# Head sums of layer 1 in three batches: by ScalarE's relu and an adding DMA in place of VectorE

## The chip, the core and the metric

The kernel runs on one core of a Trainium2 chip. Its engines are TensorE (PE in the profile, its weight loads PEld), VectorE (DVE), ScalarE (ACT), GpSimd (POOL) and SyncE (SP, which only issues transfers). Each works through its own instructions in order and waits on semaphores for the others. The metric is the device time of the whole kernel in microseconds, lower is better.

## The reference

Sixteen graphs (batches) of 1024 nodes with 128 features pass through two layers of graph attention. The change is in layer 1, whose computation is this:

```python
# x: [16, 1024, 128], adj: [16, 1024, 1024], H = 4 heads
h = jnp.einsum('bnf,hfd->hbnd', X, conv_w) + conv_b[:, None, None, :]
scores = jnp.einsum('hbni,hij,hbmj->hbnm', h, attn_w, h)
Ah = jnp.tanh(A[None] * scores)
hh = jax.nn.relu(jnp.einsum('hbnm,hbmd->hbnd', Ah, h))
Xm = jax.nn.relu(jnp.mean(hh, axis=0))
return jax.nn.relu(Xm + X)
# and around it: x = _layernorm(x + layer1(x, adj))
```

The mean over the four heads of the relu of each head's output is what this case is about. Layer 0 (masked softmax attention with three gates, then a layer norm) runs ahead of layer 1 for the next batch.

## The kernel before

Everything is 32-bit float. Layer 1 of one batch is 32 steps: 4 heads (hd) times 8 blocks of 128 nodes (m). A step s is 8*hd + m. `layer1_step` does the following in step s.

- TensorE multiplies a block of x1T with uT into two PSUM tiles `sc` of 128x512 (L704). The tag `sc` has four PSUM slots, which small tiles of layer 0 use as well.
- VectorE multiplies each with the adjacency into the SBUF tile `s`, 128x1024, of tag `s1` with four slots (L705).
- ScalarE takes the tanh of `s` in place (L706).
- TensorE accumulates the `s` of two steps earlier, with h1 as weights, into the PSUM tile `acc1`, 128x1024 (L710). The function `back` that does so waits in a list, `pending`, of length DELAY = 2. Tag `acc1` has one slot: the next head's accumulation starts after the last reader of this head's.
- After the last block of a head, which is two steps into the next head (or batch), `back` calls `add_head` for each half of 512 columns. For head 0 it writes relu(acc) into the SBUF tile `sum` (L726), for the others it adds relu(acc) to it (L728). Head 0 thus ends at step 9, head 1 at step 17, head 2 at step 25, and head 3 at step 1 of the next batch.

At step 2 of the next batch `layer1_end` transposes `sum` on VectorE (L281), writes it to DRAM and reads it back in another order through SP's queue (L263, L268), then adds x1 (L774, L775), normalises and stores the rows. `sum` has one buffer.

The order of everything is written out by hand: tables named BETWEEN and AHEAD tell after which step which piece of layer 0 of the next batches is emitted. What matters here: step 14 to 20 hold the score blocks S of layer 0 two batches ahead (L354 on TensorE, L360 on ScalarE) with their transpositions T (L378), and the gates of the next batch (sum L549 on VectorE, product L543 on GpSimd); step 25 transposes the next batch's x1 (L281) and starts the adjacency loads L0 to L7, one per step, on GpSimd's queue (L302); then come edges E (L401 on GpSimd), masks A (L418 and L426 on VectorE, the exponential L430 on ScalarE) and weightings B (L444, L451 on VectorE, L448 on ScalarE, L462 on TensorE). GpSimd issues the adjacency loads and the output stores; SP issues the rest. A slot of a tag is handed to a new tile when all reads of the old one are behind it in the program, and the first instruction that touches the new tile waits for them to be done.

Of the kernel before, what the change touches and what calls it, by code (L numbers as in the profile page):

```python
# [11 lines left out]
F32 = mybir.dt.float32  # L12
BF16 = mybir.dt.bfloat16
U8 = mybir.dt.uint8
AF = mybir.ActivationFunctionType
ALU = mybir.AluOpType
# [3 lines left out]
P = 128  # L20
# [4 lines left out]
def two_layer_adjacency_kernel(  # L25
# [19 lines left out]
    nc = tc.nc  # L45
# [9 lines left out]
    sb = ctx.enter_context(tc.tile_pool(name="sb", bufs=2))  # L55
# [631 lines left out]
    def layer1_step(b, hd, m):  # L687
# [20 lines left out]
        def back(halves=range(NH)):  # L708
            for q in halves:
                nc.tensor.matmul(  # L710
                    acc[:, ts(q, 512)], h1[:, ts(hd, D)], s[:, ts(q, 512)],
                    start=(m == 0), stop=(m == NB - 1),
                )
            if m == NB - 1:
                if hd == 0:
                    sum_t[b] = sb.tile([P, N], F32, tag="sum", name=f"sum_{b}", bufs=1)
                for q in halves:
                    add_head(b, hd, acc[:, ts(q, 512)], q * 512)
# [3 lines left out]
    def add_head(b, hd, a, at):  # L722

        o = sum_t[b][:, at : at + a.shape[1]]
        if hd == 0:
            nc.vector.tensor_scalar_max(o, a, 0.0)  # L726
        else:
            nc.vector.scalar_tensor_tensor(o, a, 0.0, o, op0=ALU.max, op1=ALU.add)  # L728
# [142 lines left out]
    for b in range(B):  # L871
        plan = BETWEEN if b else {**BETWEEN, **FIRST}
        after = layer0(b + 2) if b + 2 < B else {}
        for step in range(H * NB):
            hd, m = divmod(step, NB)
# [81 lines left out]
```

## Time and profile before

| what | value |
|---|---|
| runs | 2409.5, 2409.74, 2414.6 us; median 2409.74 |
| profiled execution | span from first to last instruction 2407.4 us; its own device time is not listed apart, the median run lies 2.3 us above the span |
| busy | PE 2398.8 us, DVE 1551.3, ACT 1063.5, POOL 608.9 |
| one batch in the steady part | 148.77 us |
| L728, add of a head's half on VectorE | 95 times, 686 ns each |
| L726, head 0's half | 32 times, 686 ns each |
| GpSimd's issue of a load of 512 KB | 590 ns; 4.1 us from issue to landing |
| granted TensorE clock | 0.999 of full speed |

How to read it: busy times are sums over the span, per engine, and say which engine has room. A line of the groups names the source line, engine, operation, what it writes and reads, how often, its busy time and mean, and then the idle time of its engine just before it with what ended that idle time. A timeline line gives the start and length in us, the engine, the line and the operation, and in brackets the idle time before it. Windows give the busy time of each engine in a stretch, then the clock, the share of time in which the 16 DMA engines were busy, and GB/s.

### The profile page before, as it was taken

To read this page: it belongs to the slowest core of one execution; us is meant where nothing else is said; L and a number is where in the kernel's file an instruction comes from. 1 tells how busy PE (TensorE), PEld (TensorE's weight loads), DVE (VectorE), ACT (ScalarE), POOL (GpSimd) and SP (SyncE) were. 2 spreads that over 40 slices of the span, in tenths; PEclk is the share of its full clock that TensorE was granted. 3 is DMA by queue.
4 is the path that set the end of the run, shared out by engine and by line. 5 is a ranking of instruction groups with operands and counts; after the bars stand their busy time and mean duration, and the time that the engine had idled before them with its cause. 6 is when DMAs were issued, how large, how long until landed. Compare 5 with 4: busy or idle time off the path is not lost.

```text
span 2407.4 us, 20166 instructions
## 1 busy us (share of the span) xinstructions
PE 2398.8 (100%) x5983; PEld 1095.6 (46%) x5983; DVE 1551.3 (64%) x3262; ACT 1063.5 (44%) x1503; POOL 608.9 (25%) x389
## 2 busy tenths in 40 slices
PE   9999999999999999999999999999999999999999
PEld 5444444444444444444444444444444444444444
DVE  7666666766667656666666666667666576666555
ACT  6545344453444534445444454444444344443333
POOL 2214131241312313133131231313214132141000
PEclk9999999999999999999999999999999999999999
DMA  5334151442414324243242422425234252341010
GB/s 192 72 78 123 46 130 42 97 106 50 126 47 104 94 60 115 53 111 82 63 113 62 115 69 70 110 56 123 62 78 108 51 131 53 80 115 34 18 27 10
DMA packets 474194, 196.98 MB, mean 82 GB/s; under 512 B 414948, under 2 KB 440291, under 8 KB 474084
## 3 DMA queue, kind: packets, MB, share of 16 engines
q1 hardware_dynamic: 455501, 129.03, 23.0%
q0 software_dynamic: 18288, 66.59, 9.3%
q8 instruction: 48, 0.79, 0.1%
q14 instruction: 63, 0.51, 0.1%
q10 hardware_dynamic: 294, 0.07, 0.0%
HBM read 136.12 MB, written 59.51 MB: 81 GB/s over the span
## 4 chain that ended last, share of the span: by engine, by line
PE 99%; DVE 1%; ACT 0%; issue 0%; POOLq 0%; DVEq 0%
PE sc L704 36%; PE acc L710 36%; PE acc L462 9%; PE sc L354 5%; PE pR L675 5%; PE pT_u L238 5%; PE pR_h L335 1%; PE pT_q L238 1%; PE acc_other L462 0%; PE idle L136 0%; DVE R L418 0%; DVE s L705 0%; PE pt L496 0%; DVE st L214 0%; PE turn L371 0%
## 5 line engine op out<-in xcount | busy, mean ns | idle before, releaser
L705 DVE TENSOR_TENSOR s<-sc,adj 128x512 f32<-128x512 f32 x1008 | 685.1, 688 | 713.9 <-PE sc L704 692.7
L706 ACT ACTIVATE s<-s 128x1024 f32<-128x1024 f32 x504 | 533.1, 1058 | 1056.9 <-DVE s L705 897.7
L704 PE MATMUL sc<-uT,x1T 128*128 128x512 f32 x2048 | 962.8, 592 | 0.2
L710 PE MATMUL acc<-s,h 128*128 128x512 f32 x2016 | 947.3, 592 | 0.0
L710 PEld LDWEIGHTS acc<-s,h 128*128 128x128 f32 x2016 | 380.5, 190 | 484.7 <-issue 476.7
L704 PEld LDWEIGHTS sc<-uT,x1T 128*128 128x128 f32 x2048 | 386.7, 190 | 470.2 <-issue 403.5
L401 POOL TENSOR_SCALAR edge<-adj 128x1024 uint8<-128x1024 f32 x120 | 332.8, 2773 | 315.3 <-DVE top_None L418 312.9
L218 POOL TENSOR_TENSOR rs<-rs,mhalf 128x8 f32<-128x8 f32 (+3 forms) x35 | 54.2, 1549 | 881.0 <-DVE rs L217 880.9
L462 PE MATMUL acc<-R,hz 128*128 128x512 f32 x492 | 231.6, 592 | 0.2 <-ACT hz L448 0.2
L430 ACT ACTIVATE R<-R,nmax 128x1024 f32<-128x1024 f32 x126 | 144.6, 1147 | 81.0 <-DVE nmax L426 73.3
L418 DVE CUSTOM_DVE_ANT_0 R<-R,edge 128x1024 f32<-128x1024 f32 x126 | 152.8, 1213 | 0.5 <-ACT hz L448 0.5
L451 DVE TENSOR_TENSOR R<-R,adj 128x1024 f32<-128x1024 f32 (+1 forms) x127 | 152.0, 1197 | 0.0
L462 PEld LDWEIGHTS acc<-R,hz 128*128 128x128 f32 x492 | 93.1, 190 | 115.7 <-issue 111.4
L354 PE MATMUL sc<-xT,qT 128*128 128x512 f32 (+3 forms) x384 | 144.9, 486 | 0.0
L360 ACT ACTIVATE R<-sc,h 128x512 f32<-128x512 f32 (+1 forms) x192 | 111.1, 580 | 52.3 <-PE sc L354 46.8
L543 POOL TENSOR_TENSOR x1T<-hp,wu_b 128x1024 f32<-128x1024 f32 x45 | 106.4, 2363 | 103.8 <-DVE hws L549 63.6
L238 PE MATMUL pT_u<-x1T,ms 128*128 128x512 f32 x256 | 120.6, 593 | 0.0
L675 PE MATMUL pR<-cw,x1T 128*128 128x512 f32 x256 | 117.6, 598 | 0.0
L354 PEld LDWEIGHTS sc<-xT,qT 128*128 128x128 f32 x384 | 69.9, 190 | 70.0 <-issue 60.6
L302 POOL DMA_DIRECT2D adj<-in_adjT_dram x112 | 66.1, 590 | 91.8 <-DVE s L705 91.8
L728 DVE SCALAR_TENSOR_TENSOR sum<-acc,sum 128x512 f32<-128x512 f32 x95 | 61.2, 686 | 41.7 <-PE acc L710 41.7
L678 ACT COPY h<-pR 128x512 f32<-128x512 f32 x128 | 72.4, 593 | 28.2 <-PE pR L675 26.4
(163 smaller groups left out, 1151.5 us busy)
## 6 DMA issues: line engine op xcount, KB each, us to landing
adj<-in_adjT_dram POOLq DMA_DIRECT2D x112, 512.0 KB, 4.1
xT<-in_xT_dram SPq DMA_DIRECT2D x16, 512.0 KB, 4.7
adj<-in_adjT_dram SPq DMA_DIRECT2D x16, 512.0 KB, 8.8
x<-in_x_dram SPq DMA_DIRECT2D x16, 512.0 KB, 5.5
dram_hp<-turn_hp SPq DMA_DIRECT2D x15, 512.0 KB, 2.6
hp<-dram_hp SPq DMA_DIRECT2D x60, 128.0 KB, 3.1
dram_x<-turn_x SPq DMA_DIRECT2D x15, 512.0 KB, 2.9
x1T<-dram_x SPq DMA_DIRECT2D x60, 128.0 KB, 5.5
```

Source lines behind the costliest of these rows:

```text
L238: nc.tensor.matmul(ps, w, src[:, ts(q, 512)], start=True, stop=True)
L354: nc.tensor.matmul(ps[:, : at - lo], t["qT"][:, ts(j, P)], t["xT"][:, lo:at], start=True, stop=True)
L401: engine.tensor_scalar(m, adj_t[b, j], 0.0, None, ALU.is_gt)
L418: nc.vector.tensor_tensor_reduce(to[:, ks], s[:, ks], t["edge", j][:, ks], 1.0, nmax, ALU.mult, ALU.max, top)
L430: nc.scalar.activation(row(j), row(j), AF.Exp, bias=t["nmax", j], accum_out=t["z", j])
L451: nc.vector.tensor_mul(s[:, ks], s[:, ks], adj[:, ks])
L462: nc.tensor.matmul(t["acc"][q], t["hz", j], row(j)[:, ts(q, BH), :], start=(j == 0), stop=(j == NB - 1),)
L675: nc.tensor.matmul(ps, x1T_t[b][:, ts(k, P)], cw.rearrange("p h d -> p (h d)"), start=True, stop=True)
L704: nc.tensor.matmul(ps, x1T[:, ts(m, P)], uT[:, ts(q, 512)], start=True, stop=True)
L705: nc.vector.tensor_mul(s[:, ts(q, 512)], ps, adj[:, ts(q, 512)])
L706: nc.scalar.activation(s, s, AF.Tanh)
L710: nc.tensor.matmul(acc[:, ts(q, 512)], h1[:, ts(hd, D)], s[:, ts(q, 512)], start=(m == 0), stop=(m == NB - 1),)
```

## The change

In batches 9, 10 and 11, for heads 1, 2 and 3, `add_head` no longer lets VectorE add. ScalarE writes relu(acc), 128x512, from PSUM into a new SBUF tile `r`, and GpSimd issues a DMA that adds `r` to the half of `sum`. `r` takes a slot of tag `s1`, the four slots that `s` uses; `r` fills half of one. Head 0 and all other batches are as before.

```diff
--- before.py
+++ after.py
@@ -722,6 +722,11 @@
     def add_head(b, hd, a, at):
 
         o = sum_t[b][:, at : at + a.shape[1]]
+        if hd and b in (9, 10, 11):
+            r = sb.tile([P, 512], F32, tag="s1", name=f"r_{b}_{hd}_{at}", bufs=4)
+            nc.scalar.activation(r, a, AF.Relu)
+            nc.gpsimd.dma_start(o, r, accum_op=ALU.add)
+            return
         if hd == 0:
             nc.vector.tensor_scalar_max(o, a, 0.0)
         else:
```

## The prediction

> **What bounds the kernel now.** I read the page's busy shares first, then its chain of waits, then the costliest groups.
>
> ```profile
> PE 2398.8 (100%) x5983; PEld 1095.6 (46%) x5983; DVE 1551.3 (64%) x3262; ACT 1063.5 (44%) x1503; POOL 608.9 (25%) x389
> PE 99%; DVE 1%; ACT 0%; issue 0%; POOLq 0%; DVEq 0%
> L728 DVE SCALAR_TENSOR_TENSOR sum<-acc,sum 128x512 f32<-128x512 f32 x95 | 61.2, 686 | 41.7 <-PE acc L710 41.7
> ```
>
> TensorE is busy throughout and the chain is 99% PE. The list of waits between 1334 and 1930 us shows no wait of PE's matmuls at all, and head 1 of batches 9, 10 and 11 reaches L728 at 1486.32, 1635.09 and 1783.85: 148.77 us apart each time, so one batch stands for all three. The times below are batch 9's. Freeing VectorE (64%) buys nothing by itself. The question is whether the change delays anything that PE needs.
>
> [...]
>
> **What goes and comes.** In batches 9 to 11, heads 1 to 3, two halves: 18 instructions of L728 leave DVE (18 x 0.686 = 12.3 us, off PE's path: worth 0). ACT gets 18 relus from PSUM; the nearest row is the same operation at L470. POOL gets 18 issues, nearest row 0.59 us of L302: 10.6 us.
>
> ```profile
> L470 ACT ACTIVATE hpT<-acc 128x512 f32<-128x512 f32 x31 | 16.9, 595 | 26.8 <-PE acc L462 26.8
> L302 POOL DMA_DIRECT2D adj<-in_adjT_dram x112 | 66.1, 590 | 91.8 <-DVE s L705 91.8
> ```
>
> ACT's 10.7 us lie in its gaps; L360 behind the relu at step 17 slips by under 1 us, and its PSUM slots aren't needed for 4 us. POOL is free at 1486.79, 1516.19 and 1553.56, before the relus of all three places. At step 25 the adj load L0, which POOL issues after the additions, waits until both additions are issued (1522.7 instead of 1516.15), so edge E0 starts near 1528 instead of 1524.5, done at 1531, before its mask at 1532.66. Cost 0 with that cover; without it that mask, and DVE behind it, would be late.
>
> **The two new waits.** r uses tag s1, four slots. A matmul of L710 comes two steps after its s (DELAY is 2). When step 18's s is allocated, those of steps 16 and 17 are still to be read, so the only slots left are those of the two r. Hence the multiply of the next step waits until the first addition has landed, the one after it for the second. And at step 2 of the next batch the transposition of sum (L281) waits for both. Behind these on DVE stands everything: L549, masks, the next multiplies; PE waits for a multiply when its score needs that PSUM slot (four slots, two per step).
>
> **Price of an addition.** It isn't in the trace. One quiet adj load, issued at 1540.14, landed at 1544.03; the windows' last columns are DMA share and GB/s:
>
> ```profile
> 1541.60:1542.10 0.50, 0.50 (x2) 0.19 (x1) 0.47 (x3) 0.00 (x0) 0.06 (x1) 1.00 0.28 49
> 1542.10:1542.60 0.50, 0.50 (x3) 0.21 (x2) 0.03 (x1) 0.43 (x1) 0.50 (x1) 1.00 0.58 221
> 1542.60:1543.10 0.50, 0.50 (x3) 0.26 (x2) 0.00 (x0) 0.50 (x1) 0.50 (x1) 1.00 1.04 426
> 1543.10:1543.60 0.50, 0.50 (x3) 0.10 (x1) 0.00 (x0) 0.50 (x3) 0.50 (x1) 1.00 0.71 287
> ```
>
> So 2.0 us pass before data flows, then about 430 GB/s, then 0.5 to the landing. 256 KB are 0.6 us a pass. Lower bound, one pass: L = 3.1 from issue to landing, the second G = 0.6 later. [...] I take L = 4.8, G = 2.3, three passes and 0.5 for the adder, of whose rate I know nothing; upper bound L = 7, G = 4, passes at under half the rate.
>
> **Place A, step 17 (head 1).** Timelines by engine, batch 9 (start, length, engine, line):
>
> ```profile
> 1485.39 1.06 ACT L706 ACTIVATE s<-s 128x1024 f32<-128x1024 f32 x1 [1.81 <-DVE s L705]
> 1488.47 0.69 DVE L705 TENSOR_TENSOR s<-sc,adj 128x512 f32<-128x512 f32 x1
> 1491.92 1.45 PE L704 MATMUL sc<-uT,x1T 128*128 128x512 f32 x3
> ```
>
> The first relu follows the tanh, done at 1486.96; POOL wakes 0.3 later, as after L705 elsewhere (mul 1519.56, L302 at 1519.86): issue 1487.26. The score at 1491.92 takes the PSUM slot that the 1488.47 multiply empties, so the landing must come by 1491.92 - 0.69 - 0.13 (semaphores, my allowance) = 1491.1: **L up to 3.85 is free**. The transposing reads keep DMA 89% busy from 1487 to 1491; +0.4. Stall 4.8 + 0.4 - 3.85 = 1.35 us. Late next on DVE are L549 and the transposition L378, by some 4 us: GpSimd's L543 at 1491.22 goes to about 1495 and ends at 1497.5, its reader is at 1498.74; SP's write and reads behind L378 feed masks that come at step 29. Both free.
>
> **Place B, step 25 (head 2).**
>
> ```profile
> 1519.65 1.06 ACT L706 ACTIVATE s<-s 128x1024 f32<-128x1024 f32 x1 [2.87 <-DVE s L705]
> 1520.03 1.29 DVE L728 SCALAR_TENSOR_TENSOR sum<-acc,sum 128x512 f32<-128x512 f32 x2 [0.47 <-PE acc L710]
> 1521.55 1.88 PE L710 MATMUL acc<-s,h 128*128 128x512 f32 x4
> 1526.70 1.88 PE L704 MATMUL sc<-uT,x1T 128*128 128x512 f32 x4
> ```
>
> DVE frees acc at 1521.32, 0.2 ahead of head 3's first matmul. The relus stand behind the tanh and end at 1521.8: PE loses 0.4. The first addition issues at 1521.5; the score at 1526.70 needs it landed by 1525.9, L up to 4.4, with 0.2 for the 512 KB write beside it: 5.0 - 4.4 = 0.6, which includes the 0.4. The second may take L + G = 7.8, and takes 7.3.
>
> **Place C, step 1 of the next batch (head 3).**
>
> ```profile
> 1557.04 1.06 ACT L706 ACTIVATE s<-s 128x1024 f32<-128x1024 f32 x1 [2.21 <-DVE s L705]
> 1562.01 1.24 DVE L281 STREAM_TRANSPOSE turn_sum<-sum 128x1024 f32<-128x1024 f32 x1
> 1573.22 1.88 PE L704 MATMUL sc<-uT,x1T 128*128 128x512 f32 x4
> ```
>
> Issue 1558.9. If L281 starts at T, DVE's queue gives L281 1.2, mask and nmax 1.3, multiply 1.3, L451 1.3, mask 1.3, and the first half of the multiply of step 4, 0.7: T + 7.2, needed at 1573.1. So T up to 1565.9, L + G up to 7.0, and it takes 7.1: 0.1. The reads of sum land 3 to 4 us later, and their reader L774 is at 1580.89: free.
>
> **Sum.** 1.35 + 0.6 + 0.1 = 2.05 us a batch, times three: +6.2. PE has no gap in which to catch up. The profiled span 2407.4 becomes 2413.6; the runs' median of 2409.74 lies 2.3 above the span, so 2415.9, say **2416**. What a measurement of this kernel can tell from no change is about 0.2%, 4.8 us.
>
> **Rivals.** *Additions land early.* The place is A: at L under 3.85 the wait is hidden, and B keeps 0.4. The sum is 3 x 0.4 = 1.2, 2410.9; up to L = 4.4, G = 1.8 it stays at 3 x (0.95 + 0.4) = 4.1, still no change. [...] It decides the sign: below L of about 4.5 no change. *The adder is slow.* L = 7, G = 4: A 3.55, B 3.4 (now by the second addition), C 4.0, 11 x 3 = 33: 2443. Nothing in the trace excludes it. *VectorE's relief shortens the chain.* The chain gives DVE 1% of the whole span and PE has no wait in these batches; at most the noise, 2409. That the change doesn't happen is excluded: every head's end in those batches goes through add_head.
>
> **Chances.** Forecast (L from 4.5 to 6) 0.45; early landing 0.36; slow adder 0.15; faster 0.04. So faster 0.04, same 0.36, slower 0.60. The range, 2410 to 2436, takes in the lower bound's 2410.9 and L = 6, G = 3.3 (A 2.55, B 1.8, C 2.3: +20, 2430) with some room; it leaves out the slowest adder and the quick end, 2 in 10.
>
> **What would show it.** In the profile after: a relu group of 18 at 0.6 us; 18 adding issues on POOL with a landing time near 4.8 to 5.2; idle time of DVE before L705 put down to those DMAs; PE waits for DVE at three places in each of three batches, and a step between batches of 150.8 instead of 148.77. Landings under 3.9 without PE waits would prove me wrong at the price; PE waits with early landings, at the slots; a gap elsewhere, at something I left out.

## The result: 6 us slower, and the profile after

| | before | after |
|---|---|---|
| median of 14 runs each, us | 2409.52 | 2415.49 |
| span of the profiled execution, us | 2407.4 | 2413.5 |
| granted TensorE clock | 0.999 | 0.999 |

The ratio is 1.0021, with a 95% interval of 1.0014 to 1.0028. The forecast was 2416.0 us. Some executions, of before and of after alike, take about 5 us longer (2414.6 and 2420.8 us), and the profiled ones of relu_only, plain_copy and quiet_place below are such, with matmuls up to twice as far apart in their first 30 us (four of L354 take 3.76 us in relu_only, 1.96 in before), so for these three I compare medians and the starts of matmuls, not spans.

These are the busy shares, the shares of the chain of waits, three groups and the landing of the additions, from the page of after.

```profile
PE 2400.4 (99%) x5983; PEld 1095.0 (45%) x5983; DVE 1544.5 (64%) x3244; ACT 1070.4 (44%) x1521; POOL 626.6 (26%) x407
PE 96%; DVE 2%; ACT 1%; DMA 1%; issue 0%; SPq 0%; POOLq 0%; DVEq 0%; ACTq 0%
L302 POOL DMA_DIRECT2D adj<-in_adjT_dram x112 | 67.6, 621 | 80.4 <-DVE s L705 80.4
L728 POOL DMA_DIRECT2D sum<-r x18 | 16.4, 1053 | 33.6 <-ACT r L727 33.6
L727 ACT ACTIVATE r<-acc 128x512 f32<-128x512 f32 x18 | 9.7, 591 | 0.0
sum<-r POOLq DMA_DIRECT2D x18, 256.0 KB, 4.3
```

The change does what it says: 18 relus of 591 ns, and 18 additions issued by POOL. DVE is 6.8 us less busy, not 12.3, which is a first hint that something else on it grew. The chain, 99% PE before, now passes through DVE, ACT and DMA for some 4%; that is the way the work was followed back, not the loss, which is 0.25% of the span. An adding issue is recorded with 1.05 us, not the 0.59 of a load's issue, but the records overlap: what stands behind an addition starts 0.55 to 0.64 us after it. From issue to landing it takes a median of 4.3 us.

The list of PE's waits over the whole span has two entries that before had not:

```profile
PE pR L675 <- ACT uT L240: 2.5, 3, 1.1
PE sc L704 <- DVE s L705: 1.6, 3, 1.0
```

The second is the wait foreseen at step 17. The first, once in each of the three batches, nobody had forecast, and it is the larger.

**Where the 6 us lie.** PE issues the same matmuls in the same order in both kernels. So I subtract each matmul's start before from its start after: past the opening the difference is constant, except at nine places, three in each changed batch.

| place | batch 9 | 10 | 11 | sum, us |
|---|---|---|---|---|
| A, step 17, head 1, L704 | 1.30 | 0.55 | 0.52 | 2.37 |
| B, step 25, head 2, L710 | 0.30 | 0.30 | 0.30 | 0.90 |
| C, head 3, step 1 to 4 of the next batch | 0 | 0 | 0 | 0 |
| E, step 31 or 32, L675 | 1.16 | 0.92 | 0.71 | 2.79 |

They sum to 6.06, the 6.1 of the spans. "Place E" is a name that the prediction doesn't have.

**Place A.** The timeline of after, batch 9 (start, length, engine, line, and in brackets the idle time before):

```profile
1492.34 1.29 DVE L705 TENSOR_TENSOR s<-sc,adj 128x512 f32<-128x512 f32 x2 [6.20 <-DMA sum<-r]
1493.09 1.98 PE L704 MATMUL sc<-uT,x1T 128*128 128x512 f32 x4 [1.03 <-DVE s L705]
```

DVE stands for 6.20 us until the first addition has landed, 4.97 us after its issue at 1487.25, and PE runs dry for the score that needs the multiply. In batches 10 and 11 the landings took 4.23 and 4.21, and PE lost 0.55 and 0.52. The loss is the landing less a fixed free time: in the eight versions, this one and seven of those below, that keep r in `s1` and move head 1's halves beside other transfers (30 landings, from 3.93 to 4.97 us), PE lost the landing less 3.67 or 3.68 us every time. The free time worked out before was 3.85, with 0.13 for the semaphores, an estimate for which no line of before was given; in after, 0.12 us pass from the landing to the multiply and 0.05 from the multiply's end to the matmul, in all three batches.

**Place C.** Here the additions land into idle DMA engines: in before, their share is 0.00 from 1556 to 1564. The windows of after cover the flight of the first addition at A and at C; the last three columns are clock, DMA share and GB/s.

```profile
1487.20:1492.20 5.00, 4.85 (x13) 1.93 (x11) 0.00 (x0) 1.17 (x3) 1.83 (x2) 1.00 1.05 173
1561.60:1565.00 3.40, 3.40 (x9) 1.52 (x8) 0.00 (x0) 0.53 (x2) 1.82 (x2) 1.00 0.57 98
```

In both windows VectorE stands still (0.00) and GpSimd does nothing but the two issues (1.83 and 1.82); what differs is the DMA share, 1.05 against 0.57. At C, with the engines otherwise idle, the first landed 3.37 us after its issue, the second 1.5 later: T lay before the 1565.9 that was free, and nothing was lost. At A, with the engines full, the same transfer took up to 4.97.

**Place E.** First GpSimd's timeline of after: the loads and edges of layer 0 two batches ahead, behind the additions of head 2.

```profile
1522.77 1.80 POOL L728 DMA_DIRECT2D sum<-r  x2 [5.31 <-ACT r L727]
1523.94 1.74 POOL L302 DMA_DIRECT2D adj<-in_adjT_dram  x2
1530.81 2.79 POOL L401 TENSOR_SCALAR edge<-adj 128x1024 uint8<-128x1024 f32 x1 [1.89 <-DMA adj<-in_adjT_dram]
1534.29 3.78 POOL L401 TENSOR_SCALAR edge<-adj 128x1024 uint8<-128x1024 f32 x1
1538.65 3.30 POOL L401 TENSOR_SCALAR edge<-adj 128x1024 uint8<-128x1024 f32 x1
1542.53 2.78 POOL L401 TENSOR_SCALAR edge<-adj 128x1024 uint8<-128x1024 f32 x1
```

L0 is issued right behind the additions, at 1523.94 instead of 1516.15, shares the DMA engines with them and lands 6.8 us later instead of 4.1; edge E0 starts at 1530.81 instead of 1524.49. Then the mask, the copy and the matmul that it delays:

```profile
1542.29 2.38 DVE L418 CUSTOM_DVE_ANT_0 R<-R,edge 128x1024 f32<-128x1024 f32 x1
1546.04 1.05 ACT L240 COPY uT<-pT_u 128x512 f32<-128x512 f32 x2
1546.66 1.98 PE L675 MATMUL pR<-cw,x1T 128*128 128x512 f32 x4 [1.06 <-ACT uT L240]
```

The same mask and the edge beside it in the timeline of before:

```profile
1540.72 1.22 DVE L418 CUSTOM_DVE_ANT_0 R<-R,edge 128x1024 f32<-128x1024 f32 x1
1542.04 2.77 POOL L401 TENSOR_SCALAR edge<-adj 128x1024 uint8<-128x1024 f32 x1 [1.30 <-DVE top_None L418]
```

In batch 9 this mask is not late. A and B had moved PE by 1.60 us, so it is due at 1542.32, and it starts at 1542.29. It is **long**: 2.38 us instead of 1.22. That is 1.16 more, which is what PE loses: ScalarE does this mask's exponential before it copies uT, so the copy and L675 come that much later. The mask begins 0.24 us ahead of an edge on GpSimd; before, that edge waited for it and began after its end.

In batches 10 and 11 the same thing happens a little earlier: two masks and a weighting are stretched, and the last mask keeps its 1.21 us but starts 0.93 and 0.71 us late, which is PE's loss there. The last two of batch 10 in after, then in before:

```profile
1692.11 1.96 DVE L451 TENSOR_TENSOR R<-R,adj 128x1024 f32<-128x1024 f32 x1
1693.99 1.21 DVE L418 CUSTOM_DVE_ANT_0 R<-R,edge 128x1024 f32<-128x1024 f32 x1
```

```profile
1688.36 1.21 DVE L451 TENSOR_TENSOR R<-R,adj 128x1024 f32<-128x1024 f32 x1
1689.48 1.22 DVE L418 CUSTOM_DVE_ANT_0 R<-R,edge 128x1024 f32<-128x1024 f32 x1
```

In all traces of this case together there are 78 pairs of an edge (L401) and a mask or weighting (L418, L451) that start within 0.6 us of each other. In 52 of them VectorE's instruction is stretched, and ends 2.11 to 2.14 us after the edge's start (one: 2.25), however early it began. In the other 26 it takes its 1.21 to 1.23, and the edge is stretched instead, to end 2.63 us after it: so the 3.78 and the 3.30 above. With starts 1.2 us apart or more, neither is. I read this as one of the two waiting for the other. Masks and weightings read two SBUF tiles. The multiply L705, which reads one of its two inputs from PSUM, is not hit: it starts within 0.6 us of an edge 683 times in these traces and never takes more than its 0.69. In the kernel before no such pair exists: the nearest starts lie 1.28 us apart. Why the two do not run side by side, the traces do not show. If the stretched one waits, it does not wait to the edge's end: by an estimate from 2.14 less the mask's own 1.22, only for its first 0.9 us of a recorded 2.78. Nor do the recorded starts tell which one is stretched: in 43 pairs VectorE's comes first, and in 17 of these it is VectorE that is stretched.

### The profile page after: what moved, and what is told of

Read it like the earlier page. It is cut to its first block, busy times and chain, and to the rows that moved or that the text cites. A ratio compares the mean times of both kernels' runs of the same rounds, so it can differ in the third digit from the quotient of the medians.

```text
span 2413.5 us, 20180 instructions
## 1 busy us (share of the span) xinstructions
PE 2400.4 (99%) x5983; PEld 1095.0 (45%) x5983; DVE 1544.5 (64%) x3244; ACT 1070.4 (44%) x1521; POOL 626.6 (26%) x407
## 4 chain that ended last, share of the span: by engine, by line
PE 96%; DVE 2%; ACT 1%; DMA 1%; issue 0%; SPq 0%; POOLq 0%; DVEq 0%; ACTq 0%
PE sc L704 36%; PE acc L710 35%; PE acc L462 9%; PE sc L354 5%; PE pT_u L238 4%; PE pR L675 4%; PE pR_h L335 1%; PE pT_q L238 1%; DVE R L418 1%; DMA sum<-r 1%; DVE s L705 0%; DVE R L451 0%; ACT R L430 0%; PE acc_other L462 0%; SPq L268 0%
## 5 line engine op out<-in xcount | busy, mean ns | idle before, releaser
L705 DVE TENSOR_TENSOR s<-sc,adj 128x512 f32<-128x512 f32 x1008 | 683.0, 688 | 733.8 <-PE sc L704 677.1
L704 PE MATMUL sc<-uT,x1T 128*128 128x512 f32 x2048 | 963.1, 592 | 1.7 <-DVE s L705 1.6
L710 PE MATMUL acc<-s,h 128*128 128x512 f32 x2016 | 947.6, 592 | 0.1
L704 PEld LDWEIGHTS sc<-uT,x1T 128*128 128x128 f32 x2048 | 386.5, 190 | 472.8 <-issue 401.6
L710 PEld LDWEIGHTS acc<-s,h 128*128 128x128 f32 x2016 | 380.5, 190 | 485.6 <-issue 474.3
L401 POOL TENSOR_SCALAR edge<-adj 128x1024 uint8<-128x1024 f32 x120 | 334.4, 2787 | 291.8 <-DVE top_None L418 283.6
L418 DVE CUSTOM_DVE_ANT_0 R<-R,edge 128x1024 f32<-128x1024 f32 x126 | 157.8, 1252 | 0.9 <-ACT hz L448 0.5
L451 DVE TENSOR_TENSOR R<-R,adj 128x1024 f32<-128x1024 f32 (+1 forms) x127 | 153.5, 1210 | 0.0
L354 PE MATMUL sc<-xT,qT 128*128 128x512 f32 (+3 forms) x384 | 144.9, 486 | 0.0
L238 PE MATMUL pT_u<-x1T,ms 128*128 128x512 f32 x256 | 120.6, 593 | 0.0
L675 PE MATMUL pR<-cw,x1T 128*128 128x512 f32 x256 | 117.9, 598 | 2.5 <-ACT uT L240 2.5
L354 PEld LDWEIGHTS sc<-xT,qT 128*128 128x128 f32 x384 | 69.9, 190 | 70.1 <-issue 60.6
L240 ACT COPY uT<-pT_u 128x512 f32<-128x512 f32 x128 | 71.5, 581 | 20.0 <-PE pT_u L238 20.0
```

The lines of the kernel that those rows point to most:

```text
L238: nc.tensor.matmul(ps, w, src[:, ts(q, 512)], start=True, stop=True)
L354: nc.tensor.matmul(ps[:, : at - lo], t["qT"][:, ts(j, P)], t["xT"][:, lo:at], start=True, stop=True)
L401: engine.tensor_scalar(m, adj_t[b, j], 0.0, None, ALU.is_gt)
L418: nc.vector.tensor_tensor_reduce(to[:, ks], s[:, ks], t["edge", j][:, ks], 1.0, nmax, ALU.mult, ALU.max, top)
L451: nc.vector.tensor_mul(s[:, ks], s[:, ks], adj[:, ks])
L675: nc.tensor.matmul(ps, x1T_t[b][:, ts(k, P)], cw.rearrange("p h d -> p (h d)"), start=True, stop=True)
```

## The experiments

The losses are read as above, from the starts of the same matmuls against before. The medians of before beside them are 2409.3 to 2409.7.

**relu_only**: the relu on ScalarE stays, VectorE adds from SBUF, no DMA.

```diff
-            nc.gpsimd.dma_start(o, r, accum_op=ALU.add)
+            nc.vector.tensor_add(o, o, r)
```

> ScalarE's relu into r in s1 as in the change, but VectorE adds r to sum from SBUF; no adding DMA. Theory: only the 0.9 us at step 25 stay, span 2408.3. Rival (the relus on ScalarE and the lost slots, rather than the landing, cost the time): 2410 to 2413.5.

Measured: 2410.41 us, ratio 1.0004 (0.9998 to 1.0011). PE loses 0.30 at B in each batch, 0.9 in all, and nothing at A, C or E. The list of waits of PE's weight loads in these batches:

```profile
PEld acc L710 <- ACT r L727: 2.6, 3, 0.9
```

So B is the relus behind the tanh alone, and all else is the DMA's doing. This run doesn't price VectorE's relief, since VectorE still adds. That the relief was worth nothing is read from after: past the opening none of its matmuls gains on before by more than 0.05 us, and heads_1_3 below, which has two thirds of the relief, gains nowhere either.

**heads_1_3** and **head_2**: the change for two of the heads, and for the third.

```diff
-        if hd and b in (9, 10, 11):
+        if hd in (1, 3) and b in (9, 10, 11):    # heads_1_3
+        if hd == 2 and b in (9, 10, 11):         # head_2
```

> The change for heads 1 and 3 alone; head 2 stays on VectorE. Theory: 2.4 us at step 18, nothing at step 2 of the next batch, nothing at step 25 to 31: span 2409.8. Rival (the wait of the transposition of sum at step 2 costs too, hidden in the sum so far): 2411 or more, with a PE wait between steps 3 and 6.

> The change for head 2 alone. Theory: 0.9 us from the relus behind the tanh and 2.8 from the late adjacency loads and edges, span 2411.1; no PE wait at step 18. Rival (the wait at L675 needs the delay that head 1 left on VectorE and GpSimd): 2408.3.

Measured: heads_1_3 2412.1 us, 1.0009 (1.0002 to 1.0015): A 0.91, 0.92, 0.90, nothing elsewhere. head_2 2412.85 us, 1.0011 (1.0005 to 1.0018): B 0.9, E 1.17, 0.53 and 0.59, nothing at A. Its PE waits:

```profile
PE pR L675 <- ACT uT L240: 2.0, 3, 1.1
```

2.73 and 3.19 sum to 5.9 of 6.06: the losses add up, and E belongs to head 2 alone.

**load_ahead**: head 2's additions are issued after the load L0 of the same step instead of ahead of it. Nothing else moves.

```diff
+            if hd == 2:
+                late.append((o, r))
+            else:
+                nc.gpsimd.dma_start(o, r, accum_op=ALU.add)
...
             run(after, AHEAD.get(step, ""))
+            while late:
+                nc.gpsimd.dma_start(*late.pop(0), accum_op=ALU.add)
```

> The whole change, but at step 25 the two additions are issued on POOL behind the first adjacency load L0 instead of ahead of it; nothing else moves. Theory (L0, held behind the additions and then moving its data beside them, lands late, so the edges, masks and ScalarE's uT copy are late and PE waits at L675 for 2.8 us in all): L0 lands before 1522, E0 starts about 2 us earlier, the wait at L675 goes or falls under 0.3 a batch: span 2413.5 - 2 to 2.8 = 2411. Rival (the multiply of step 26, held by r's slot, makes L2 and with it the edges late): the wait at L675 stays above 0.6 a batch.

Measured: 2413.36 us, 1.0014 (1.0006 to 1.0022). E is gone, but for 0.3 us at another matmul in one batch; B stays 0.9, A is 2.81. GpSimd's and VectorE's timelines:

```profile
1517.00 0.63 POOL L302 DMA_DIRECT2D adj<-in_adjT_dram  x1
1539.40 2.76 POOL L401 TENSOR_SCALAR edge<-adj 128x1024 uint8<-128x1024 f32 x1 [0.65 <-DMA adj<-in_adjT_dram]
1541.86 1.22 DVE L418 CUSTOM_DVE_ANT_0 R<-R,edge 128x1024 f32<-128x1024 f32 x1
```

L0 is out at 1517.00 again and lands 4.05 us later, the mask starts 2.5 us into an edge and takes its 1.22. No mask or weighting is stretched in this whole trace; after has seven, head_2 seven, and heads_1_3 no pair of an edge with one of them that start within 0.6 us. E's cause is thus the place of the load in GpSimd's queue, by way of the edges that it moves onto the masks.

**plain_copy**: the DMA writes r over the half of sum instead of adding it.

```diff
-            nc.gpsimd.dma_start(o, r, accum_op=ALU.add)
+            nc.gpsimd.dma_start(o, r)
```

> The DMA copies r over the half of sum instead of adding it, so sum keeps the last head's part only; everything else as in the change. It prices the adding itself. Theory [...]: landing 3.4 to 3.7 us at step 17 instead of 4.2 to 5.0, PE's wait at step 18 gone or under 0.3 a batch, span about 2407.4 + 3.5 = 2410.9. Rival (adding costs nothing, the latency is the queue's and the issue's): landings and span as in the change, 2413.5.

Measured: 2413.54 us, 1.0017 (1.0009 to 1.0024). In its groups the issue is recorded with 0.58 us:

```profile
L728 POOL DMA_DIRECT2D sum<-r x18 | 10.4, 580 | 33.5 <-ACT r L727 33.5
```

At C the first copy lands after 2.33, 2.33 and 2.38 us, where an addition took 3.37: the adding costs **1.04 us** in quiet. The DMA queue of GpSimd during the two transfers at C of batch 9, in after (window 1561.5 to 1567.0) and in plain_copy (1565.9 to 1570.0), with packets, MB and share of the 16 engines:

```profile
q0 software_dynamic: 288, 0.52, 55.8%
q0 software_dynamic: 160, 0.52, 33.9%
```

An addition moves the same 256 KB as 128 packets of 2 KB, the copy as 64 of 4 KB (16 small ones besides), and a packet takes about as long, 189 against 172 ns. So the adding doubles the time of the DMA engines, from 0.7 to 1.5 us for each transfer spread over 16 engines, and the first packet starts 1.5 us after the issue, not 1.2. At A copies take 4.76, 4.15 and 4.86 (DMA share 0.93 in batch 9) and PE loses 2.73, as much as with additions. So at A it isn't the adding that sets the landing but what flies beside it. At B and E the copies cost 1.20 and 0.85: behind them L0 lands after 5.2 to 5.5 us instead of 6.8 to 7.0, and two masks are stretched.

**reads_later**: SP's transposing reads of step 17 are left to a later step, so that they don't fly with head 1's additions.

```diff
-            land()
+            if not (b in (9, 10, 11) and step == 17):
+                land()
```

> The whole change, but in batches 9 to 11 the four transposing reads that SP issues at step 17 are issued one step later, behind the next write, so that fewer transfers run beside the additions of head 1. Theory (at step 17 the landing of 4.2 to 5.0 us, against 3.4 where the DMA engines are idle, is shared DMA time, and the copy without adding landed no sooner): first landing 3.4 to 4.0 us, PE's wait at step 18 under 0.3 a batch, span 2413.5 - 2 = 2411.5. Rival (the landing is the price of adding behind GpSimd's own work): landing and wait as in the change.

Measured: 2414.64 us, 1.0019 (1.0011 to 1.0026). The landings at A were 4.47, 4.37 and 4.16 us, not quiet: SP's write of 384 KB now goes out first, and the reads follow from 1486.68 on, still beside the additions. A 1.98, B 0.9, E 1.73. It doesn't tell the theories apart.

**quiet_place** is the better form of it: load_ahead, and in batches 9 to 11 the transpositions T0 to T6 of layer 0 come two steps later, the score blocks S staying where they are, so that at step 17 nothing flies at all.

```diff
...
+    LATER = {
+        **AHEAD, 16: "S1", 17: "S2", 18: "T0 S3", 19: "T1 S4", 20: "T2 S5", 21: "T3 S6",
+        22: "T4 S7", 23: "T5", 24: "T6",
+    }
...
-            run(after, AHEAD.get(step, ""))
+            run(after, (LATER if b in (9, 10, 11) else AHEAD).get(step, ""))
```

> The load L0 ahead of the additions at step 25 as in the run before, and in batches 9 to 11 the transpositions T0 to T6 of layer 0, with SP's writes and reads, come later (steps 18 to 24 instead of 16 to 22), so that nothing else uses the DMA engines when head 1's additions are issued at step 17. Theory (the landing at step 17 is shared DMA time): first landing 3.4 to 3.7 us as at step 1, PE's wait at step 18 gone, only the relus behind the tanh left: span 2408.3 to 2409, no change that can be measured against the kernel before. Rival (the landing at step 17 is the adding behind GpSimd's and VectorE's own work there): 4.2 to 5.0 us, PE wait of 0.8 a batch, span 2411.

Measured: 2436.52 us, 1.0103 (1.0086 to 1.012). The landing at A is 3.45, 3.34 and 3.38, and A is **gone**: with a DMA share of 0.59 in batch 9, where after had 1.05, the landing is as short as at C, so it is the shared DMA engines that made it late. But the whole is much worse, by PE's waits, DVE's and PE's timelines and a window with the clock (0.50) in the third column from the end:

```profile
PE acc L710 <- ACT r L727: 13.0, 3, 4.5
1528.89 0.31 DVE L378 STREAM_TRANSPOSE turn<-R 128x128 f32<-128x128 f32 x1 [3.72 <-DMA dram_turn<-turn]
1532.55 3.46 PE L710 MATMUL acc<-s,h 128*128 128x512 f32 x4 [4.53 <-ACT r L727]
1533.50:1535.80 2.30, 2.30 (x3) 0.75 (x3) 1.25 (x1) 0.00 (x0) 1.13 (x2) 0.50 0.95 157
```

The last transposition now waits 3.72 us for a write to leave its buffer; behind it on DVE stand the multiply of the step, then ScalarE's tanh, then the relus, and PE waits 4.2 to 4.5 us in each batch for acc1. After each of these waits the granted clock reads 0.50; in batch 9 the four matmuls from 1532.55 on take 3.46 us and the next four 2.14, where 1.88 is usual, which costs about 1.8 us more, and 1.5 to 2.0 us are lost again where uT is made (L238). In the kernel before, VectorE has no wait for such a write in these batches.

**both_moved**: load_ahead and reads_later together.

> Both moves. Theory: only the relus behind the tanh at step 25 are left, 0.9 us, at most 1.5: span 2408.3 to 2409, no change that can be measured against the kernel before. Rival (the waits move on to another place, as when r had a slot of its own): 2410 or more.

Measured: 2412.64 us, 1.0008 (1.0001 to 1.0014), the least of all versions with additions in three heads: A 2.35, B 0.9, E 0. The expectation missed, since A stays.

**own_slot**: r gets a slot that no multiply needs.

```diff
...
-            r = sb.tile([P, 512], F32, tag="s1", name=f"r_{b}_{hd}_{at}", bufs=4)
+            if at == 0:
+                r_t[b] = sb.tile([P, N], F32, tag="uT1", name=f"r_{b}_{hd}")
+            r = r_t[b][:, at : at + a.shape[1]]
```

> r takes a free slot of tag uT1 (one 128x1024 tile for both halves) instead of two slots of s1; additions and their place in POOL's queue as in the change. Theory (the change's 6.1 us are 2.4 from the next multiply waiting for r's slot in s1 at step 18, 0.9 from the relus behind the tanh at step 25, 2.8 from the adjacency loads and edges that POOL starts late behind the additions at step 25): the wait at step 18 goes, the others stay, span 2407.4 + 3.7 = 2411.1. Rival (all but the 0.9 comes from VectorE held by r's slot, the late masks at step 27 to 31 too): 2407.4 + 0.9 = 2408.3, no PE wait left at L675.

Measured: 2416.16 us, 1.0024 (1.0014 to 1.0034). A is gone, as the theory of the slots has it, but nothing is gained: B is 3.16 and E 3.36. No multiply waits for r here, so E doesn't come from the slots. Its PE waits and a transposition ahead of step 25:

```profile
PE pR L675 <- ACT uT L240: 3.0, 3, 1.2
PE acc L710 <- ACT r L729: 2.4, 3, 1.0
1512.10 0.31 DVE L378 STREAM_TRANSPOSE turn<-R 128x128 f32<-128x128 f32 x1 [0.79 <-DMA dram_turn<-turn]
```

Counted from each run's opening, PE now reaches step 25 of batch 9 1.3 us earlier than in after, while the transpositions, bound to their DMAs, do not; the multiply, the tanh and the relus come late relative to PE. In before and after no transposition waits there. In after, A's stall had covered this; that is read from the order on VectorE, no run isolates it. So a stall taken away uncovers the next one.

**sp_loads** and **own_slot_sp**: the loads L0 and L1 of batches 11 to 13 go to SP's queue, alone and with own_slot.

```diff
-            (nc.sync if b < 2 else nc.gpsimd).dma_start(a, adjT[b, ts(j, P), :])
+            (nc.sync if b < 2 or (b in (11, 12, 13) and j < 2) else nc.gpsimd).dma_start(a, adjT[b, ts(j, P), :])
```

> The whole change, but the two adjacency loads L0 and L1 at steps 25 and 26 of batches 9 to 11 are issued from SP's queue, so they don't stand behind the additions. Theory (POOL's order makes edges, masks and so ScalarE's uT copy late): the PE wait at L675 goes, span 2413.5 - 2.8 = 2410.7. Rival (VectorE held by r's slot makes the masks late): the wait at L675 stays, 2413.5.

> Both: r in a slot of uT1, and L0 and L1 from SP's queue. Theory: only the relus behind the tanh are left, 0.9 us, span 2408.3, no change that can be measured. Rival (a further wait takes the place of those removed, such as L2 on POOL or the reads of sum): 2410 or more.

Measured: 2423.01 us, 1.0059 (1.0046 to 1.0071), and 2428.51 us, 1.0077 (1.0063 to 1.0091): both missed. SP's queue and PE in sp_loads:

```profile
1524.87 5.23 SPq L268 DMA_DIRECT2D x1T<-dram_x  x4
1530.20 0.62 SPq L302 DMA_DIRECT2D adj<-in_adjT_dram  x1
1529.08 1.98 PE L704 MATMUL sc<-uT,x1T 128*128 128x512 f32 x4 [1.20 <-DVE s L705]
```

L0 now flies beside head 2's additions, whose landing goes from 3.8 to 4.3 in after to 5.99, 6.76 and 7.78 us, and the score at step 28 waits, 6.9 us in all; L1 stands behind four reads of x1T in SP's queue until 1530.20, and its edge is late; E is still 2.15. The load slowed the additions though it came from another queue. In own_slot_sp B is 4.1 and E 17.4: L1 leaves SP's queue at 1533.23, its edge and then PE stand waiting, and in two of the three batches the clock reads 0.50 around this, and the four matmuls below take 3.78 us. GpSimd's and PE's timelines:

```profile
1539.60 2.76 POOL L401 TENSOR_SCALAR edge<-adj 128x1024 uint8<-128x1024 f32 x1 [7.46 <-DMA adj<-in_adjT_dram]
1549.50 3.78 PE L675 MATMUL pR<-cw,x1T 128*128 128x512 f32 x4 [3.03 <-ACT uT L240]
```

**nine_batches**: the change in batches 3 to 11.

```diff
-        if hd and b in (9, 10, 11):
+        if hd and 3 <= b <= 11:
```

> The change in batches 3 to 11, nine instead of three. Theory with the cost of the later batches (1.55 to 1.8 us each): 2407.4 + 14 to 16 = 2421.5 to 2423.5. If every batch cost what batch 9 did (2.76): 2432. If the costs hide behind each other after some batches: under 2418.

Measured: 2434.58 us, 1.0104 (1.009 to 1.0118). By the matmuls 23.1 us, 2.6 a batch, where 14 to 16 were expected from batches 10 and 11. The losses do not settle: single batches cost from 1.1 to 3.8 us, their mean is near the 2.76 of batch 9, and 19 masks and weightings are stretched.

No version is faster than the kernel before. The nearest, relu_only, is not to be told from it.

## Why the prediction was right, and where it was not

The direction, the size and the first cause were right: PE stalls because DVE waits for the landing. But that the sum of 6.2 came out at 6.06 was luck, for two errors cancelled: A, B and C were put 2.9 us too high (6.15 against 3.27), and E, put at nothing, cost 2.79. Without place E the loss would have been 3.3 us, within the 0.2% that was called no change. The 2.3 us put between span and median are 1.8 within one execution (2415.29 and 2413.5), which is most of what 2416.0 is above 2415.49.

- **That the additions' wait and price decide**: right. 18 additions, the wait at the very multiply named, and a free time of 3.67 at A where 3.85 was worked out, in every landing. own_slot, without that wait, has no loss at A.
- **Price of an addition, L = 4.8, G = 2.3**: too high in quiet, where L is 3.37 and the second lands 1.5 later. Beside other transfers, at A and B, it lands 2.4 to 2.8 later. About half of the error in L is in the fixed part: one pass was put at 3.1, read from a load from DRAM, and the plain copy landed after 2.33. The other half is the adding, put by estimate at two more passes of 0.6 and 0.5 for the adder, 1.7, where it costs 1.04. The DMA engines' time doubles, from 0.7 to 1.5 us a transfer; what fills the second half of it, the traces don't show. The rival of early landings had the better quiet price.
- **Contention at A, +0.4**: too low. It is 4.97, 4.23 and 4.21 less 3.37: 1.6, 0.9 and 0.8, and quiet_place removes it. These two errors partly cancel; A is 2.37 for three batches where 4.05 was forecast, since batches 10 and 11 land 0.7 us earlier than batch 9. One batch's times do not stand for all three there. A landing at A also varies by itself: up to step 17 of batch 9 after, heads_1_3, load_ahead and sp_loads are the same program, and they land after 4.97, 4.58, 4.51 and 4.36.
- **Place B, 0.6**: 0.30 each. Of its parts only the relus behind the tanh exist, 0.3 for 0.4; relu_only shows it. The landing, 3.8 to 4.3, stayed within the 4.4 that was free.
- **Place C, 0.1**: 0, since the landing is quiet there.
- **"Cost 0 with that cover", for L0 and edge E0**: this step failed, and cost 2.79 us. The cover named did hold: E0 ended at 1533.60, before its mask at 1534.22. E0's start was put near 1528, which A and B make 1529.6; it was 1530.81, since the load's 4.1 us became 6.8 beside the additions. What failed is the conclusion from "edge done before its mask" to "free". The later edges then began together with masks and weightings, and in each such pair one is stretched, the mask of batch 9 from 1.22 to 2.38 us; load_ahead removes the loss. The longer record of an adding issue has no part in it: L0's issue starts 1.17 us after the first addition's, in plain_copy 1.16 after the first copy's.
- **12.3 us less on VectorE, worth 0**: right, since no matmul of after gains on before. In after the 12.3 us left, and the seven stretched instructions (14.8 us in all instead of 8.5) gave some 6 back.
- **Distance of batches 150.8**: for batch 9 to 10, matmuls at A are 148.77 plus B, E and the next A apart, 150.8; right, by the wrong terms.

Open is what sets a single landing at A: with a spread of 0.6 us between executions of the same program, the 0.7 between batches may be no more than that, and differences of A between versions that all have full DMA engines there say little. Open too is why edges and masks collide: what is measured is that one of them is stretched, and by how much, and no run had the same edges on another engine.

## What to carry to other kernels

When an instruction is put into a queue, follow everything behind it in that queue to its next meeting with another engine, not only to its first reader: here a load 8 us later cost more by whom its edges met than by when they were done. Price a DMA with what flies beside it: the same addition took 3.4 us alone and 5.0 in a full place, and the adding was the small part, 1.04 us in quiet. Read a loss from the starts of the same matmuls in two traces, place by place; a sum that fits can hide two errors, and a stall removed can uncover the one behind it.

## What was new of the hardware

- An adding DMA of 256 KB between SBUF tiles: 3.37 us from issue to landing in quiet against 2.33 of a plain copy, with twice the packets of half the size at about the same time each; its issue is recorded with 0.9 to 1.2 us against 0.6, yet what stands behind it on GpSimd starts after 0.55 to 0.64 us, as behind a plain one.
- An edge (L401 on GpSimd, an SBUF tile to another) and a mask or weighting (L418 or L451 on VectorE, two SBUF tiles) that start within 0.6 us of each other: one is stretched, in after the mask or weighting from 1.2 us to between 1.92 and 2.38, or the edge from 2.78 to 3.30 and 3.78.
- After PE's stalls of 4.2 to 4.5 us in quiet_place the granted clock reads 0.50: four matmuls took 3.0 to 3.5 us instead of 1.88, with starts up to 0.85 apart instead of 0.43, about 1.8 us more in each batch. The stalls of 1.3 us and less in after show no such slowing: four matmuls take 1.98 us right behind those of 1.03 and 1.06. In own_slot_sp a shorter stall of 3.03 us went with a reading of 0.50 in two batches and not in the third. How long a stall has to be for it is not shown.
